# Row-LSTM over a group-normalised image: statistics laid out on 128 partitions, the first block's loads moved up among the first chunks, and the first row normalised on two other engines

## The chip, the cores and the metric

The kernel runs on one core of a Trainium2 chip. A core has a matrix engine (TensorE, PE in the profile; its weight loads are PEld), a vector engine (VectorE, DVE), an activation engine (ScalarE, ACT), a general engine (GpSimd, POOL) and a sync engine (SyncE, SP) that here only issues transfers. Sixteen DMA engines move data between the device memory (HBM) and the on-chip SBUF; PSUM takes the products of TensorE. Each engine works through its own instructions in order and waits on semaphores for the others. The metric is device time in microseconds (us); lower is better.

## The reference

The input `x` has shape (8, 96, 128, 128): batch, channels, rows, columns, in fp32. It is group-normalised, run row by row through a convolutional LSTM, and added to the result.

```python
def _gn(v, G=32, eps=1e-5):
    g = v.reshape(B_, G, C_ // G, H_, W_)
    m = jnp.mean(g, axis=(2, 3, 4), keepdims=True)
    s = jnp.var(g, axis=(2, 3, 4), keepdims=True)
    return ((g - m) / jnp.sqrt(s + eps)).reshape(v.shape)
...
its = conv(X, W_is * mask, padding=((0, 0), (1, 1))) + b_is       # 96 -> 384 channels, 3 wide, causal mask
def step(carry, row_in):                                          # over the 128 rows
    ss = conv(h, W_ss, padding=((1, 1),)) + b_ss                  # 96 -> 384 channels, 3 wide
    gates = ss + row_in
    ...
    c_new = f * c + i * g
    h_new = o * jnp.tanh(c_new)
...
x = x + _L0_conv_ref(_gn(x), ...)
```

Two facts matter here. The mean and the variance of a group (3 channels of one image, 49152 contiguous numbers) must be known before the first row can be normalised, so all 50.33 MB of `x` have to be read once before the recurrence starts. And the recurrence is serial: row r+1 needs the `h` of row r.

## The kernel before, in words

**Stage 1, statistics.** For each of the 8 images the kernel reads `x[b]` as 96 channels on 96 partitions, in 8 chunks of 2048 columns (768 KB, line 139, tile `xc`, 64 chunks in all). The chunks go through four buffers: the pool `x_pool` has the tags x0 and x1 with two buffers each. VectorE takes four `bn_stats` of 512 columns from each chunk (line 141, tile `bst`) and one `bn_aggr` for each image (line 142, tile `st`).

**Stage 2, from statistics to scale and shift.** Tiny products with the 0/1 matrix `gm` on TensorE (line 155) add the channels of a group and spread the sum to the partitions in the two layouts that are needed later; VectorE and ScalarE turn them into `rstd` and `nmr` (lines 158 to 172).

**Stage 3, the first block.** The batch is cut in two halves (s = 0 and 1, four images each) and the rows into blocks of R = 4. For each half and block `load_rows` reads channels 0 to 63 twice into `xr` (partitions 0 to 63, one float further on, and 64 to 127; lines 183 and 184, 512 KB each), and `load` reads channels 64 to 95 and 0 to 95 into an `x` tile (lines 189 and 190, 256 and 768 KB). SyncE issues these in program order behind the chunks. GpSimd then normalises the whole block of four rows, 8 instructions for each half (line 194: into `xn` from `xr`, and into the lower 32 partitions of `hx` from `x`), and clears a border column (line 213).

**Stage 4, the recurrence.** 128 rows times two halves give 256 half-steps. In a half-step TensorE makes 15 products in fp32 (line 270): six 256 columns wide on `vs` and `vf`, three 512 wide on `xn`, six 256 wide on `vd`. ScalarE copies and applies sigmoid and tanh, VectorE does the sums and gates and prepares `vs` and `vf` of the next row (lines 241 and 242), GpSimd prepares `vd` (line 243), adds the residual (line 332) and normalises the next block a little in each half-step. The two halves alternate so that the gates of one lie beside the products of the other.

**What sets the order.** From the `with tc.manual_schedule` on, TensorE, ScalarE, VectorE and GpSimd run their instructions in the order in which the code names them. Everything ahead of it is put in order by the framework's scheduler; SyncE's transfers keep program order on their queue. A DMA takes one of eight semaphores in turn and waits until the earlier DMA on that semaphore has landed.

Of the kernel before, what the change touches and what calls it, by code (L numbers as in the profile page):

```python
# [11 lines left out]
GROUPS = 32  # L12
# [9 lines left out]
def kernel(  # L22
# [38 lines left out]
    HW = H * W  # L61
    CH = R * BH * W
    SN = 512
    GSZ = C // GROUPS
# [43 lines left out]
    gm = const.tile([C, 2, P], F32, name="gm")  # L108
# [24 lines left out]
    st = const.tile([C, B, 2], F32, name="st")  # L133
    for b in range(B):
        bst = g_pool.tile([C, HW // SN, 6], F32, tag="bst", name=f"bst{b}")
        xb = x[b].rearrange("c h w -> c (h w)")
        for k in range(HW // CH):
            xc = x_pool.tile([P, CH], F32, tag=f"x{(b * (HW // CH) + k) % 2}", name=f"xc{b}_{k}")
            nc.sync.dma_start(xc[0:C], xb[:, bass.ts(k, CH)])
            for j in range(CH // SN):  # L140
                nc.vector.bn_stats(bst[:, k * (CH // SN) + j, :], xc[0:C, bass.ts(j, SN)])  # L141
        nc.vector.bn_aggr(st[:, b, :], bst.rearrange("c n s -> c (n s)"))


    mean = const.tile([P, 2, B], F32, name="mean")
    dq = const.tile([C, 2, B], F32, name="dq")
    v = const.tile([P, 2, B], F32, name="v")
    t1 = const.tile([P, 2, B], F32, name="t1")
    rstd = const.tile([P, 2, B], F32, name="rstd")
    nmr = const.tile([P, 2, B], F32, name="nmr")  # L150

    def grouped(src):
        pm = ps_st.tile([P, 2, B], F32, tag="pst", name="pm")
        for i in range(2):
            nc.tensor.matmul(pm[:, i, :], gm[:, i, :], src, start=True, stop=True)  # L155
        return pm

    nc.vector.tensor_copy(dq[:, 0, :], st[:, :, 0])  # L158
    nc.vector.tensor_scalar_mul(mean, grouped(dq[:, 0, :]), 1.0 / GSZ)
    nc.vector.tensor_sub(dq[:, 1, :], dq[:, 0, :], mean[0:C, 0, :])  # L160
    nc.vector.tensor_mul(dq[:, 1, :], dq[:, 1, :], dq[:, 1, :])
    nc.vector.tensor_add(dq[:, 1, :], dq[:, 1, :], st[:, :, 1])
    nc.vector.tensor_scalar(v, grouped(dq[:, 1, :]), 1.0 / GSZ, GN_EPS, ALU.mult, ALU.add)
    nc.scalar.activation(t1, v, AF.Sqrt)
    nc.vector.reciprocal(rstd, t1)

    nc.vector.tensor_mul(t1, rstd, rstd)
    nc.vector.tensor_mul(t1, t1, v)
    nc.vector.tensor_scalar(t1, t1, -0.5, 1.5, ALU.mult, ALU.add)
    nc.vector.tensor_mul(rstd, rstd, t1)  # L170
    nc.vector.tensor_mul(nmr, mean, rstd)
    nc.vector.tensor_scalar_mul(nmr, nmr, -1.0)  # L172


# [18 lines left out]
    def norm(dst, src, lo, layout, b):  # L193
        nc.gpsimd.tensor_scalar(  # L194
            dst,
            src,
            rstd[lo:P, layout, b : b + 1],
            nmr[lo:P, layout, b : b + 1],
            ALU.mult,
            ALU.add,  # L200
        )

    def normalise_own(s, k, j):

        i = k % 2
        norm(
            xn[s][i][:, :, :, j, :],
            xr[s][:, j, 0 : R * W].rearrange("p (r j t) -> p r t j", r=R, t=2),
            0,
            1,  # L210
            s * BH + j,
        )
        nc.gpsimd.memset(xn[s][i][0:C2, :, 0, j, 0:1], 0.0)

    def normalise_shared(s, k, j):

        norm(
            strided(
                hx[s][k % 2][C:P, 0, 0, j, :], 0, [(2 * BH * JP, R), (BH * JP + 1, 2), (1, J)]
            ),  # L220
            xt[s, k][C:P, j, :, :].rearrange("p r (j t) -> p r t j", t=2),
            C,
# [242 lines left out]
```

## Time and profile before

| what | value |
|---|---|
| median of three runs | 2238.5 us (2235.78 to 2239.08) |
| the profiled execution's own time | 2246.42 us |
| its span (first to last instruction) | 2244.6 us |
| instructions | 24459 |
| bytes read from HBM / written | 185.39 MB / 50.33 MB |
| busy share of the span | PE 89%, DVE 73%, PEld 64%, ACT 60%, POOL 46% |

The profile is one execution, taken by the hardware profiler. Its page shows each engine's busy share in 40 slices of about 56 us, the chain of work that ended last, and the costliest groups of instructions with what ended the idle time before them. A stretch can be looked at by itself: the table of stretches gives for each its length, the busy time of each engine with the count of instructions, the clock granted to TensorE, the mean busy share of the 16 DMA engines (1.00 and a little over mean that all are occupied all the time) and the rate in GB/s. The timeline gives instructions with their start and duration. Each fp32 product of the code is two MATMUL records.

### The profile page before, as it was taken

The numbers are of one execution on the slowest core, as the hardware profiler recorded it, in microseconds if no ns is written. First come the engines' busy times: TensorE is split into PE (matmuls) and PEld (weight loads), VectorE is DVE, ScalarE is ACT, GpSimd is POOL, SyncE is SP. The second block draws the span as 40 slices with busy tenths as digits, with TensorE's granted clock in tenths as the row PEclk, the third lists the DMA queues.
The fourth block names the chain that finished last, engine by engine and source line by source line (L and its number), as shares of the span: only waits on it lengthen the run. The fifth ranks groups of instructions, "written<-read, shape, count | busy, mean of one in ns | idle before, by whom it ended". The sixth has DMA issues, their size and how long they took to land.

```text
span 2244.6 us, 24459 instructions
## 1 busy us (share of the span) xinstructions
PE 2002.9 (89%) x7688; PEld 1441.8 (64%) x7688; DVE 1629.4 (73%) x3354; ACT 1348.8 (60%) x2564; POOL 1027.0 (46%) x1311
## 2 busy tenths in 40 slices
PE   0000899999999999999999999999999999999998
PEld 0000677777777777777777777777777777777775
DVE  6787577777777777777777777777777777777776
ACT  0000566666666666666666666666666666666665
POOL 0000545554555554455555555445555555544552
PEclk9999999999999999999999999999999999999999
DMA  9999544333334444433333444443333344444310
GB/s 237 242 246 236 101 104 104 89 81 81 81 83 104 104 103 104 104 85 84 79 80 87 104 104 103 103 104 85 81 81 79 89 104 104 104 103 104 85 48 28
DMA packets 103520, 237.30 MB, mean 106 GB/s; under 512 B 6560, under 2 KB 7136, under 8 KB 97248
## 3 DMA queue, kind: packets, MB, share of 16 engines
q1 hardware_dynamic: 102400, 234.91, 45.2%
q8 instruction: 62, 1.02, 0.2%
q10 hardware_dynamic: 992, 0.84, 0.2%
q14 instruction: 66, 0.54, 0.1%
HBM read 185.39 MB, written 50.33 MB: 105 GB/s over the span
## 4 chain that ended last, share of the span: by engine, by line
PE 89%; DMA 7%; DVE 3%; POOL 0%; issue 0%; ACT 0%; POOLq 0%; DVEq 0%
PE ps L270 89%; DMA xc<-in_x_dram 7%; DVE bst L141 2%; DMA wt<-in_w_ss_dram 0%; DMA wt<-in_w_is_dram 0%; POOL hx L194 0%; POOL xn L194 0%; PE pm L155 0%; POOLq L460 0%; POOL x L332 0%; DVE ps L287 0%; ACT L300 0%; ACT g L296 0%; ACT ps L300 0%; DVE ps L286 0%
## 5 line engine op out<-in xcount | busy, mean ns | idle before, releaser
L270 PEld LDWEIGHTS ps<-vd,wt 128*128 128x128 f32 x3072 | 583.7, 190 | 407.2 <-issue 366.9
L270 PE MATMUL ps<-xn,wt 128*128 128x512 f32 x1536 | 795.5, 599 | 0.0
L270 PE MATMUL ps<-vd,wt 128*128 128x256 f32 x3072 | 788.4, 379 | 0.0
L296 ACT ACTIVATE g<-ps 32x512 f32<-32x512 f32 x768 | 454.2, 591 | 466.3 <-PE ps L270 466.1
L243 POOL TENSOR_TENSOR vd<-hx 128x512 f32<-128x512 f32 x256 | 266.1, 1039 | 942.4 <-DVE vf L242 748.5
L280 ACT ACTIVATE m<-ps,bias 128x256 f32<-128x256 f32 x768 | 358.6, 467 | 184.1 <-PE ps L270 184.1
L270 PE MATMUL ps<-vs,wt 128*128 128x256 f32 x1536 | 458.5, 380 | 11.6 <-DVE vs L241 11.6
L270 PE MATMUL ps<-vf,wt 128*128 128x256 f32 x1536 | 458.2, 380 | 0.0
L300 ACT ACTIVATE ps<-ps 96x512 f32<-96x512 f32 x768 | 442.9, 577 | 16.1
L304 DVE TENSOR_TENSOR ps<-ps,c 96x512 f32<-96x512 f32 x256 | 177.9, 695 | 377.8 <-ACT ps L300 377.8
L287 DVE TENSOR_TENSOR ps<-m,ps 128x256 f32<-128x256 f32 x768 | 329.2, 429 | 26.4
L286 DVE TENSOR_TENSOR ps<-m,ps 128x256 f32<-128x256 f32 x768 | 324.3, 422 | 21.4 <-ACT m L280 5.4
L332 POOL TENSOR_TENSOR x<-x,hx 96x512 f32<-96x512 f32 x256 | 331.4, 1295 | 9.5 <-DVE hx L325 9.5
L270 PEld LDWEIGHTS ps<-vs,wt 128*128 128x128 f32 x1536 | 292.5, 191 | 52.0 <-DVE vs L241 12.1
L270 PEld LDWEIGHTS ps<-vf,wt 128*128 128x128 f32 x1536 | 292.7, 191 | 40.1
L270 PEld LDWEIGHTS ps<-xn,wt 128*128 128x128 f32 x1536 | 271.1, 189 | 73.1 <-DVE ps L287 32.0
L194 POOL TENSOR_SCALAR xn<-xr,rstd,nmr 128x512 f32<-128x512 f32 x256 | 208.1, 813 | 212.1 <-DVE nmr L172 212.1
L307 DVE TENSOR_TENSOR g<-ps,g 96x512 f32<-96x512 f32 x256 | 175.6, 686 | 106.7 <-ACT g L296 106.7
L194 POOL TENSOR_SCALAR hx<-x,rstd,nmr 32x512 f32<-32x512 f32 x256 | 207.7, 811 | 25.4
L155 PE MATMUL pm<-dq,gm 96*128 96x8 f32 x8 | 2.0, 362 | 220.0 <-DVE dq L158 219.1
L141 DVE BATCH_NORM_STATS2 bst<-xc 96x6 f32<-96x512 f32 x256 | 157.4, 675 | 40.5 <-DMA xc<-in_x_dram 40.5
L325 DVE TENSOR_TENSOR hx<-ps,th 96x512 f32<-96x512 f32 x256 | 173.9, 679 | 0.7 <-ACT th L315 0.7
(41 smaller groups left out, 596.6 us busy)
## 6 DMA issues: line engine op xcount, KB each, us to landing
xr<-in_x_dram SPq DMA_DIRECT2D x128, 512.0 KB, 9.3
xc<-in_x_dram SPq DMA_DIRECT2D x64, 768.0 KB, 10.3
x<-in_x_dram SPq DMA_DIRECT2D x64, 768.0 KB, 9.6
out_dram<-x SPq DMA_DIRECT2D x64, 768.0 KB, 5.3
x<-in_x_dram SPq DMA_DIRECT2D x64, 256.0 KB, 6.3
wt<-in_w_ss_dram ACTq DMA_DIRECT2D x2, 144.0 KB, 7.4
wt<-in_w_is_dram ACTq DMA_DIRECT2D x2, 96.0 KB, 6.3
wr<-in_w_ss_dram ACTq DMA_DIRECT2D x1, 144.0 KB, 8.9
```

Of the source, the lines that this page charges most:

```text
L141: nc.vector.bn_stats(bst[:, k * (CH // SN) + j, :], xc[0:C, bass.ts(j, SN)])
L194: nc.gpsimd.tensor_scalar(dst, src, rstd[lo:P, layout, b : b + 1], nmr[lo:P, layout, b : b + 1], ALU.mult, ALU.add,)
L243: diff = nc.gpsimd.tensor_sub(vd.rearrange("p t (b j) -> p t b j", b=BH), strided(h[:, 0, 0, :], 1, [(BH * JP - 1, 2), (JP, BH), (1, J)]), ...
L270: nc.tensor.matmul(o, wt[:, p, bass.ts(a, P)], rhs, start=start, stop=stop, skip_group_check=True)
L280: nc.scalar.activation(self.m1, self.ps[a][:, 0:HB], AF.Identity, bias=bias[:, a : a + 1])
L286: nc.vector.tensor_add(lo, self.m1, hi)
L287: nc.vector.tensor_sub(hi, self.m1, hi)
L296: nc.scalar.activation(self.g[a * 32 : (a + 1) * 32], self.ps[a][C:P], AF.Tanh)
L300: nc.scalar.activation(gate, gate, AF.Sigmoid)
L304: nc.vector.tensor_mul(f, f, cs[self.s].rearrange("p t b j -> p (t b j)"))
L307: nc.vector.tensor_mul(self.g, self.ps[1][0:C], self.g)
L332: nc.gpsimd.tensor_add(xo, xo, h)
```

## The change

Statistics. `x[b]` is read as a flat array cut into 128 equal pieces, one for each partition: a group is four neighbouring partitions, and an image is 6 chunks of 128 x 2048 (1 MiB), 48 chunks in all. The four chunk buffers are the first buffer of each `x_pool` tag and the two `xn` tiles of the odd blocks, which are not needed yet. After the fourth chunk the loads of the first block are issued. `bn_stats` and `bn_aggr` run on 128 partitions; `gm` has a third part, which gives the mean back to the 128 pieces.

First row. Row 0 of the first block is normalised ahead of rows 1 to 3: half 0 on VectorE, half 1 on ScalarE; rows 1 to 3 stay with GpSimd, behind the first `vd` of both halves. A sigmoid on one column, whose result nobody reads, comes right behind the square root.

Products that nobody reads. `spin(rows, count)` issues products 256 columns wide of the weight tile `wt` with itself, with 128, 64 or 32 rows; 112 of them stand ahead of the mean's products, ten behind the variance's.

```diff
-    gm = const.tile([C, 2, P], F32, name="gm")
+    gm = const.tile([P, 3, P], F32, name="gm")
...
-            xc = x_pool.tile([P, CH], F32, tag=f"x{(b * (HW // CH) + k) % 2}", name=f"xc{b}_{k}")
-            nc.sync.dma_start(xc[0:C], xb[:, bass.ts(k, CH)])
-                nc.vector.bn_stats(bst[:, k * (CH // SN) + j, :], xc[0:C, bass.ts(j, SN)])
...
+    ring = [
+        x_pool.tile([P, CH], F32, tag=f"x{s}", name=f"xs{s}") for s in range(NH)
+    ] + [xn[s][1].rearrange("p r t b j -> p (r t b j)") for s in range(NH)]
+    for b in range(B):
+        bst = g_pool.tile([P, QW // SN, 6], F32, tag="bst", name=f"bst{b}")
+        xb = x[b].rearrange("c h w -> (c h w)").rearrange("(p q) -> p q", p=P)
+        for k in range(QW // CH):
+            xc = ring[n % len(ring)]
+            n += 1
+            nc.sync.dma_start(xc, xb[:, bass.ts(k, CH)])
+            for j in range(CH // SN):
+                nc.vector.bn_stats(bst[:, k * (CH // SN) + j, :], xc[:, bass.ts(j, SN)])
+            if n == len(ring):
+                for s in range(NH):
+                    load_rows(s, 0)
+                    load(s, 0)
+        nc.vector.bn_aggr(st[:, b, :], bst.rearrange("c n s -> c (n s)"))
...
+    def spin(rows, count):
...
+        for i in range(count):
+            for q in range(P // rows):
+                at = bass.ds(q * rows, rows)
+                nc.tensor.matmul(
+                    banks[(q * rows // 32 + i % (rows // 32)) % 4][:, 0:256],
+                    wt[at, 0, 0:P],
+                    wt[at, 0, 0:256],
...
-    for s in range(NH):
-        load_rows(s, 0)
-        load(s, 0)
-    for s in range(NH):
-        for j in range(BH):
-            normalise_own(s, 0, j)
-            normalise_shared(s, 0, j)
-    for s in range(NH):
-        load_rows(s, 1)
-        load(s, 1)
-    moving = [inputs(s, 0) for s in range(NH)]
+    for count in (12, 4):
+        for rows in (P, 64, 32):
+            spin(rows, count)
     with tc.manual_schedule(engines={E.PE, E.Activation, E.DVE, E.Pool}):
+        for i in (2, 0, 1):
+            nc.tensor.matmul(pm[:, i, :], gm[:, i, :], st[:, :, 0], start=True, stop=True)
...
+        for i in range(2):
+            nc.tensor.matmul(pv[:, i, :], gm[:, i, :], dq, start=True, stop=True)
+        spin(P, 10)
...
+        nc.scalar.activation(t1, v, AF.Sqrt)
+        nc.scalar.activation(table, t1[:, 0, 0:1], AF.Sigmoid)
...
+        for s, engine in enumerate((nc.vector, nc.scalar)):
+            for j in range(BH):
+                normalise_shared(engine, s, 0, j, 0, 1)
+            for j in range(BH):
+                normalise_own(engine, s, 0, j, 0, 1)
+        for s in range(NH):
+            nc.vector.memset(xn[s][0][0:C2, 0, 0, :, 0:1], 0.0)
+            moving.append(inputs(s, 0))
+        for s in range(NH):
+            for j in range(BH):
+                normalise_shared(nc.gpsimd, s, 0, j, 1, R)
+            for j in range(BH):
+                normalise_own(nc.gpsimd, s, 0, j, 1, R)
+                border(nc.gpsimd, s, 0, j, 1, R)
+        for s in range(NH):
+            load_rows(s, 1)
+            load(s, 1)
```

**SyncE's transfers.** In the kernel before, the loads of the first block (`xr` and `x`, last eight rows here) stand behind the 64th chunk:

```order
L139 DMA xc_5_511<-in_x_dram 96x2048
L139 DMA xc_6_517<-in_x_dram 96x2048
L139 DMA xc_7_523<-in_x_dram 96x2048
L183 DMA xr_111<-in_x_dram 64x4x512
L184 DMA xr_111<-in_x_dram 64x4x512
L189 DMA x_0_558<-in_x_dram 32x4x512
L190 DMA x_0_558<-in_x_dram 96x4x512
L183 DMA xr_112<-in_x_dram 64x4x512
L184 DMA xr_112<-in_x_dram 64x4x512
L189 DMA x_0_563<-in_x_dram 32x4x512
L190 DMA x_0_563<-in_x_dram 96x4x512
```

After the change they stand behind the fourth chunk of 48 (the chunk buffers are `xs_129`, `xs_130`, `xn_108` and `xn_110`):

```order
L165 DMA xn_108<-in_x_dram 128x2048
L165 DMA xn_110<-in_x_dram 128x2048
L142 DMA xr_111<-in_x_dram 64x4x512
L143 DMA xr_111<-in_x_dram 64x4x512
L148 DMA x_0_155<-in_x_dram 32x4x512
L149 DMA x_0_155<-in_x_dram 96x4x512
L142 DMA xr_112<-in_x_dram 64x4x512
L143 DMA xr_112<-in_x_dram 64x4x512
L148 DMA x_0_160<-in_x_dram 32x4x512
L149 DMA x_0_160<-in_x_dram 96x4x512
L165 DMA xs_129<-in_x_dram 128x2048
L165 DMA xs_130<-in_x_dram 128x2048
```

So the fifth chunk is the thirteenth transfer of SyncE's queue, and nothing but chunks follows until the statistics end.

**GpSimd between the statistics and the recurrence.** Before, the four rows of half 0 (`xn_107`, `hx_103`) are normalised ahead of the first `vd`:

```order
L194 TENSOR_SCALAR xn_107<-xr_111,rstd,nmr 128x8x64 x2
L213 MEMSET xn_107 64x4
L194 TENSOR_SCALAR xn_107<-xr_111,rstd,nmr 128x8x64
L213 MEMSET xn_107 64x4
L194 TENSOR_SCALAR xn_107<-xr_111,rstd,nmr 128x8x64
L213 MEMSET xn_107 64x4 x2
L194 TENSOR_SCALAR hx_103<-x_0_558,rstd,nmr 32x4x2x64 x4
L243 TENSOR_TENSOR vd_0_602<-hx_103 128x512
```

After, VectorE has the first row of half 0 (half 1's stands on ScalarE in the same form), right behind the shift `nmr`:

```order
L403 TENSOR_SCALAR nmr<-nmr 128x16
L208 TENSOR_SCALAR hx_103<-x_0_155,rstd,nmr 32x2x64 x4
L208 TENSOR_SCALAR xn_107<-xr_111,rstd,nmr 128x2x64 x4
L413 MEMSET xn_107 64x4
L254 TENSOR_TENSOR vs_0_595<-hx_103 128x256
L255 TENSOR_TENSOR vf_0_596<-hx_103 128x256
L413 MEMSET xn_109 64x4
L254 TENSOR_TENSOR vs_0_602<-hx_105 128x256
```

Eight instructions of 128 columns on VectorE now stand where eight of 512 columns stood on GpSimd; GpSimd keeps the other three rows of both halves, behind its two `vd`.

**TensorE up to the first half-step**, after the change (the last two of the 112, the products for mean and variance, and the first two of the ten):

```order
L185 MATMUL spin_32_1_523<-wt 128x256
L185 MATMUL spin_32_1_524<-wt 128x256
L385 MATMUL pm<-st,gm 128x8 x3
L391 MATMUL pv<-dq,gm 128x8 x2
L185 MATMUL spin_128_0_554<-wt 128x256
L185 MATMUL spin_128_0_555<-wt 128x256
```

Before, `L155 MATMUL pm<-dq,gm 128x8 x4` is followed by the first real product, `vs` of half 0, directly; now that product comes behind the ten. The 112 need only the weight tile, which lands in the first microseconds; the ten stand between the variance's products and the first half-step.

115 lines of the change are left out of this document (59 added, 56 removed).

## The prediction, written before the result was known

> **What bounds the kernel now.** I read the page's slices first, then the chain of waits by engine.
>
> ```profile
> span 2244.6 us, 24459 instructions
> PE   0000899999999999999999999999999999999998
> DVE  6787577777777777777777777777777777777776
> DMA  9999544333334444433333444443333344444310
> PE 89%; DMA 7%; DVE 3%; POOL 0%; issue 0%; ACT 0%; POOLq 0%; DVEq 0%
> ```
>
> There are two kernels in one. From the fifth slice on TensorE is the chain; before it TensorE does nothing, the DMA engines are full, and VectorE is not. The table of stretches (length, busy time by engine, granted clock, DMA share, GB/s) puts numbers to both.
>
> ```profile
> core 0: us, PE busy (x) PEld busy (x) DVE busy (x) ACT busy (x) POOL busy (x), PEclk, DMA share, GB/s
> 1.00:2.00 1.00, 0.00 (x0) 0.00 (x0) 0.00 (x0) 0.00 (x0) 0.95 (x4) 1.00 0.69 98
> 20.00:200.00 180.00, 0.00 (x0) 0.00 (x0) 144.20 (x232) 0.00 (x0) 0.00 (x0) 1.00 1.02 246
> 400.00:1000.00 600.00, 600.00 (x2309) 432.13 (x2309) 439.19 (x924) 403.59 (x769) 306.07 (x383) 1.00 0.40 92
> ```
>
> Between 400 and 1000 us TensorE is busy for 600 of 600 us, and the change touches none of its products there. So the time can only move ahead of the recurrence. In the statistics all 16 DMA engines are occupied (1.02) and deliver 246 GB/s, while VectorE works 144 of 180 us: the transfers are the bound. The chain of waits shows the beat, four `bn_stats` in 2.48 us and then waiting for a chunk, and the timeline shows what follows the last chunk.
>
> ```profile
> 11.30 0.57 DVE wr L98
> 22.86 9.80 DMA xc<-in_x_dram
> 191.06 10.08 DMA xc<-in_x_dram
> 201.16 2.48 DVE bst L141 x4
> 215.30 2.48 DVE bst L141 x4
> 217.80 1.03 DVE st L142
> 219.07 1.02 PE L155 MATMUL pm<-dq,gm 96*128 96x8 f32 x4 [219.07 <-DVE dq L158]
> 220.13 0.17 DVE L159 TENSOR_SCALAR mean<-pm 128x16 f32<-128x16 f32 x1 [1.11 <-PE pm L155]
> 221.04 0.99 PE L155 MATMUL pm<-dq,gm 96*128 96x8 f32 x4 [0.95 <-DVE dq L162]
> 222.07 0.17 DVE L163 TENSOR_SCALAR v<-pm 128x16 f32<-128x16 f32 x1 [1.18 <-PE pm L155]
> 222.28 0.21 ACT L164 ACTIVATE t<-v 128x16 f32<-128x16 f32 x1 [210.06 <-DVE v L163]
> 223.65 0.17 DVE L171 TENSOR_TENSOR nmr<-mean,rstd 128x16 f32<-128x16 f32 x1
> 223.85 0.17 DVE L172 TENSOR_SCALAR nmr<-nmr 128x16 f32<-128x16 f32 x1
> 224.21 1.56 POOL L194 TENSOR_SCALAR xn<-xr,rstd,nmr 128x512 f32<-128x512 f32 x2 [212.12 <-DVE nmr L172]
> 231.17 0.43 DVE L241 TENSOR_TENSOR vs<-hx 128x256 f32<-128x256 f32 x1 [7.14 <-POOL hx L194]
> 231.65 1.22 PE L270 MATMUL ps<-vs,wt 128*128 128x256 f32 x2 [9.62 <-DVE vs L241]
> 236.93 1.27 PE L270 MATMUL ps<-xn,wt 128*128 128x512 f32 x2
> 237.67 1.28 ACT L296 ACT_TABLE_LOAD   x1
> 239.71 1.28 ACT L300 ACT_TABLE_LOAD   x1
> 244.52 0.70 PE L270 MATMUL ps<-vs,wt 128*128 128x256 f32 x2 [2.01 <-DVE vs L241]
> 252.47 0.59 PE L270 MATMUL ps<-vs,wt 128*128 128x256 f32 x2
> 252.90 0.59 PE L270 MATMUL ps<-vf,wt 128*128 128x256 f32 x2
> ```
>
> Call 217.8, the end of the last `bn_stats`, T. The aggregate, mean, variance and scale take until T + 6.2; GpSimd's eight normalisations until T + 13.4; the first half-step starts at T + 13.85, the second at T + 26.7 and the third at T + 34.7. The second to the third is 7.95 us; the first to the second is 12.87. In the first, six products take 231.65 to 236.93, 0.88 us each, where they later take 0.43 (252.47 to 252.90), although the granted clock reads 1.00 in every stretch shown; and ScalarE loads two tables of 1.28 us that the third half-step no longer has.
>
> **The change, part by part.** (1) *The rate of the chunks.* The same 50.33 MB come as 48 transfers of 1.049 MB over 128 partitions instead of 64 over 96. The engines are all occupied already, so is there anything to gain? The stretches of the first block's loads, which follow each other on one queue, answer that: in this order channels on partitions 0 to 63 (one float off), 64 to 127, 96 to 127, 0 to 95. The last row lies in the recurrence, where the only transfer left in flight is a store from 96 partitions, issued at 309.88.
>
> ```profile
> 210.30:213.80 3.50, 0.00 (x0) 0.00 (x0) 2.47 (x4) 0.00 (x0) 0.00 (x0) 1.00 1.05 167
> 213.80:216.30 2.50, 0.00 (x0) 0.00 (x0) 1.00 (x2) 0.00 (x0) 0.00 (x0) 1.00 1.07 211
> 216.30:217.60 1.30, 0.00 (x0) 0.00 (x0) 1.30 (x3) 0.00 (x0) 0.00 (x0) 1.00 1.07 200
> 217.60:221.00 3.40, 1.02 (x4) 0.92 (x4) 2.01 (x7) 0.00 (x0) 0.00 (x0) 1.00 1.08 236
> 319.50:320.00 0.50, 0.50 (x2) 0.19 (x1) 0.50 (x2) 0.50 (x1) 0.00 (x0) 1.00 1.05 410
> 309.88 0.59 SPq L335 DMA_DIRECT2D out_dram<-x  x1
> 321.88 0.32 SPq L189 DMA_DIRECT2D x<-in_x_dram  x1
> ```
>
> Every stretch has the engines full, and the rate goes from 167 to 410. So the share is not the limit: an engine's packets just take longer. 64 partitions of the upper half of SBUF get 211, and 32 of the same half get 200: it is the half that is worth about 205, not the count. 96 partitions, two thirds of whose bytes go to the lower half, could then get 205 x 3/2 = 308 and do get 236 to 246. 128 partitions load both halves alike: up to 2 x 205 = 410, which is also what the engines do in the store. The bounds are 246 (nothing gained) and 410; I take 400, since the halves' rows speak for the upper end.
>
> [...]
>
> (2) *When the statistics end.* Data start near 1.5 to 2 us. The first four chunks and the weights (4.2 + 0.9 MB) take 12.8 us at 400. Then come the eight loads of the first block, 4.19 MB, whose four rows above sum to 10.7 us for one half, 21 us for both; they used to run beside stages 1 to 3 and now hold up the fifth chunk. VectorE starts at about 11.3 us as before (its first instruction needs the weights), has done four chunks near 24 us, as in the row of 22.86, and waits until 2 + 12.8 + 21 + 2.6 + about 1 for landing = 39. From there 44 chunks go by the slower of two: VectorE, 2.48 + about 0.05 for the wait + a sixth of an aggregate (1.03 x 144/192 = 0.8, so 0.13) = 2.66; the transfers, 1.049/400 = 2.62. With 2.66, T becomes 39 + 117 = 156; with some unevenness between two such equal partners I take **157, a gain of 61** against 217.8. Four chunks may be in flight, 10 us of transfers against a landing time of about 2, so the ring doesn't bind.
>
> (3) *From T to the first product.* Aggregate 0.8; mean 1.6 (1.10 before with four records, now six of 0.25); up to the variance's products 0.9 and these 1.0 as before; to `nmr` 1.96 as before. Sum T + 6.3, against 6.2. Then eight instructions of 128 columns on VectorE: no row has that form; 16 columns go in steps of 0.21 (223.85 to 224.03), 256 in 0.43, so 1.7 to 3.4, and I take 1.7, as 128 columns are nearer to the small ones; border and `vs` 0.6. TensorE could start at T + 8.6, 5.3 earlier than before. The page has the two groups that price what ScalarE and GpSimd get.
>
> ```profile
> L280 ACT ACTIVATE m<-ps,bias 128x256 f32<-128x256 f32 x768 | 358.6, 467 | 184.1 <-PE ps L270 184.1
> L194 POOL TENSOR_SCALAR hx<-x,rstd,nmr 32x512 f32<-32x512 f32 x256 | 207.7, 811 | 25.4
> ```
>
> ScalarE loads the sigmoid's table (1.28) while VectorE works out `nmr`, then needs 8 x 0.34 (between the 0.21 of 222.28 and the 0.47 of a copy of 256 columns) for half 1, done by T + 9.1; half 1's first product is not due until T + 19, so this costs nothing, and the two table loads leave the first half-step. GpSimd's other 16 instructions (0.8 x 3/4 each, with eight borders, 11 us) end near T + 23; what queues behind them is `vd` of row 1, wanted near T + 30. The second block's `xr` waits for them and lands near T + 25 and T + 30, while GpSimd normalises it from T + 27 and T + 35. All this is covered by a few us each.
>
> (4) *The products that nobody reads.* The 112 wait for weights alone, so they run from about 9 us, at most 112 x 0.88 = 99 us, and are over long before T; they neither help nor hurt. The ten start at T + 4.3 and stand ahead of the real ones. If TensorE speeds up after 5.3 us of work, as in the rows of 231.65 and 236.93, six of them take 5.3 and four 1.7: the first real product moves from T + 8.6 to T + 11.3, but its half-step then runs without the slow six and takes about 7.85. Third half-step: 11.3 + 2 x 7.85 = T + 27.0. Without the ten: 8.6 + 5.3 + 5.2 + 7.9 = T + 27.0 too. They are worth nothing either way; if they stayed slow throughout, they would cost 1.6 more.
>
> [...]
>
> Sum: the third half-step stood at 217.8 + 34.7 = 252.5 and will stand at 157 + 27.0 = 184; **68.5 us** less, of them 61 from the statistics and 7.7 from the chain behind. All that follows is TensorE's own 7.8 us per half-step. The profiled execution took 2246.42 and would take 2178; its median is 7.9 lower (2238.5), so I forecast **2170 us**.
>
> **The rivals.** *Loads have a ceiling of their own.* No load in the rows above passes 246 and only a store shows 410; if each 32 partitions add what the step from 64 (205) to 96 (246) adds, 128 get 287. Then 44 chunks of 3.65 and the first four at that rate put T at 2 + 17.8 + 21 + 161 + 3.5 = 205.3: a gain of 12.5 + 7.7, 2218 us. For it: the 96-partition rate is 80% of what the halves allow. Against it: 32 and 64 partitions being equal. [...] *The rate stays, and the first block is in the way.* The place is SyncE's queue: if full engines mean 246 whatever the partitions, T = 2 + 20.7 + 21 + 187.5 + 3.5 = 235, 17 later, less 7.7 from the chain: 2248, slower. It decides below a rate of about 260, where the chunks no longer pay for the 21 us. For it: the share of 1.02; against it: the 410. *The chain behind the statistics gains nothing*, because two engines now normalise beside GpSimd, which slows VectorE's eight, and the ten stay slow: 2178 with the forecast's statistics; this lies inside the range.
>
> **How the numbers follow.** Forecast (a rate of 360 or more, the chain's rival included) 0.72, 2160 to 2185; the ceiling 0.18, 2183 to 2218; the kept rate 0.10, 2230 to 2250. I leave out the last and the upper part of the ceiling: 2160 to 2206. About 0.2% (4.5 us) is what can be told from no change here. Faster takes the first two cases, 0.90; the third splits into 0.02 the same and 0.08 slower.
>
> **What would show it.** Right: `bn_stats` without waits from about 40 us on, a rate near 390 there, an idle VectorE between 24 and 39 us, the last `bn_stats` near 157, the first real product 11 us later at the fast pace, two table loads ahead of it. Wrong: a rate below 300 with the share still at 1.0 (a ceiling), a fifth chunk that lands after 45 us (the first block slower than its rows), or a gap on TensorE in the first ten half-steps (GpSimd or `xr` late).

## The result, and the profile after

| kernel | median of its runs | span of the profiled execution | its own time |
|---|---|---|---|
| before | 2238.28 us (2235.78 to 2239.08, 4 runs) | 2244.6 | 2246.42 |
| changed | 2173.69 us (2172.96 to 2174.94, 4 runs) | 2171.9 | 2173.67 |

The ratio is 0.9714 with a 95% interval of 0.9697 to 0.9731: the change makes the kernel 64.6 us faster, and the time is 3.7 above the forecast of 2170. The page of the changed kernel, slices and chain of waits:

```profile
span 2171.9 us, 24875 instructions
PE   4019999999999999999999999999999999999998
DVE  4987777777777777777777777777777777777776
PEclk8559999999999999999999999999999999999999
DMA  9991444333444443334444332344443334444411
PE 92%; DVE 0%; issue 0%; POOLq 0%; POOL 0%; ACT 0%
```

Before, TensorE's digits rose in the fifth slice; now they rise at the end of the third, from about 154 us on. The 4 in its first slice are the products that nobody reads. Behind that the page is the old one. The table of stretches has the first block's loads and then the chunks:

```profile
18.00:34.00 16.00, 13.12 (x168) 10.99 (x164) 4.78 (x9) 0.00 (x0) 0.00 (x0) 1.00 1.06 213
...
60.00:120.00 60.00, 0.00 (x0) 0.00 (x0) 59.86 (x101) 0.00 (x0) 0.00 (x0) 0.50 1.01 420
```

At the same share of about 1.0 the engines deliver 213 GB/s to the first block and 420 to the chunks, where the kernel before had 246. VectorE is busy for 59.86 of 60 us: it and the transfers are now bounds together. The timeline from the first chunk behind the first block to the third half-step (its columns are start, duration, engine, line, and in brackets the idle time and who ended it):

```profile
41.51 4.97 DVE L167 BATCH_NORM_STATS2 bst<-xs 128x6 f32<-128x512 f32 x8 [18.73 <-DMA xs<-in_x_dram]
142.20 4.83 DVE L167 BATCH_NORM_STATS2 bst<-xs 128x6 f32<-128x512 f32 x8
150.50 2.48 DVE L167 BATCH_NORM_STATS2 bst<-xn 128x6 f32<-128x512 f32 x4 [1.09 <-DMA xn<-in_x_dram]
153.87 1.45 PE L385 MATMUL pm<-st,gm 128*128 128x8 f32 x6 [122.75 <-DVE st L172]
157.07 6.28 PE L185 MATMUL spin<-wt 128*128 128x256 f32 x20
159.23 0.17 DVE L398 TENSOR_TENSOR t<-rstd 128x16 f32<-128x16 f32 x1 [1.26 <-ACT table L395]
160.49 1.51 DVE L208 TENSOR_SCALAR hx<-x,rstd,nmr 32x128 f32<-32x128 f32 x4
162.02 1.12 DVE L208 TENSOR_SCALAR xn<-xr,rstd,nmr 128x128 f32<-128x128 f32 x4
163.75 0.67 PE L283 MATMUL ps<-vs,wt 128*128 128x256 f32 x2 [0.39 <-DVE vs L254]
171.88 0.59 PE L283 MATMUL ps<-vs,wt 128*128 128x256 f32 x2
179.73 0.59 PE L283 MATMUL ps<-vs,wt 128*128 128x256 f32 x2
```

VectorE waits 18.73 us for the fifth chunk and has its last statistics at 150.50 + 2.48 = 153.0. This is T; it was 217.8. The first real product stands at T + 10.8, the third half-step at T + 26.75 = 179.73, where it stood at 252.47: 72.7 us earlier, which is the difference of the two spans. The medians differ by 64.6 only. The experiment on the kernel before shows where half of the other 8 went, and bears on the rest.

### The profile page after: what moved, and what is told of

Read it like the earlier page. It is cut to its first block, busy times and chain, and to the rows that moved or that the text cites. A ratio compares the mean times of both kernels' runs of the same rounds, so it can differ in the third digit from the quotient of the medians.

```text
span 2171.9 us, 24875 instructions
## 1 busy us (share of the span) xinstructions
PE 2030.3 (93%) x7934; PEld 1465.1 (67%) x7934; DVE 1588.7 (73%) x3299; ACT 1351.5 (62%) x2572; POOL 1028.0 (47%) x1311
## 3 DMA queue, kind: packets, MB, share of 16 engines
HBM read 185.49 MB, written 50.33 MB: 109 GB/s over the span
## 4 chain that ended last, share of the span: by engine, by line
PE 92%; DVE 0%; issue 0%; POOLq 0%; POOL 0%; ACT 0%
PE ps L283 92%; DVE hx L208 0%; POOLq L508 0%; POOL x L345 0%; DVE ps L300 0%; DVE ps L299 0%; DVE xn L208 0%; DVE hx L338 0%; DVE c L324 0%; ACT m L293 0%; DVE vs L254 0%; DVE nmr L402 0%; DVE rstd L401 0%; DVE nmr L403 0%; DVE t L399 0%
## 5 line engine op out<-in xcount | busy, mean ns | idle before, releaser
L313 ACT ACTIVATE ps<-ps 96x512 f32<-96x512 f32 x768 | 442.9, 577 | 16.1
L208 POOL TENSOR_SCALAR hx<-x,rstd,nmr 32x512 f32<-32x512 f32 (+1 forms) x256 | 207.9, 812 | 25.4
L208 POOL TENSOR_SCALAR xn<-xr,rstd,nmr 128x512 f32<-128x512 f32 (+1 forms) x256 | 208.3, 814 | 0.2
L324 DVE TENSOR_TENSOR c<-ps,g 96x512 f32<-96x512 f32 x256 | 173.9, 679 | 0.0
L328 ACT ACTIVATE th<-c 96x512 f32<-96x512 f32 x256 | 157.9, 617 | 0.9 <-DVE c L324 0.9
```

What stands on the lines that cost most here:

```text
L208: engine.tensor_scalar(dst, src, scale, shift, ALU.mult, ALU.add)
L313: nc.scalar.activation(gate, gate, AF.Sigmoid)
L324: nc.vector.tensor_add(c, self.ps[0][0:C], self.g)
```

## The experiments

All kernels below compute the whole result, and none leaves work out. The diffs are excerpts: `...` marks what is left out, and the comments in them are added here. Where nothing else is said, the edit is made on the changed kernel, and a ratio is against the kernel before in runs of the same chip.

### The layout alone

The kernel before with the statistics on 128 partitions (48 chunks, the four old buffers), and nothing else of the change: the first block stays behind the chunks and with GpSimd, and there are no unread products.

```diff
-            nc.sync.dma_start(xc[0:C], xb[:, bass.ts(k, CH)])
+            nc.sync.dma_start(xc, xb[:, bass.ts(k, CH)])      # xb = x[b] as 128 equal pieces
```

> The kernel before with the statistics on 128 partitions and nothing else: chunks through its own four buffers, first block behind the last chunk, GpSimd normalising the whole block, no unread products. Theory (the layout alone lifts the rate from 246 to about 418 GB/s, VectorE becomes the bound): last bn_stats near 135 us, third half-step 34.7 us later as before, so 170 us against 252 before and 180 in the changed kernel: 2164 us, faster than the whole change. Rival (the layout gives the 61 to 65 us of the statistics stage only together with the early block): 2178 to 2182 us.

Measured: 2165.05 us (2164.35 to 2165.95), ratio 0.9661 (0.9638 to 0.9683). From its timeline, the last statistics and the first two half-steps:

```profile
133.62 2.47 DVE L142 BATCH_NORM_STATS2 bst<-xc 128x6 f32<-128x512 f32 x4 [2.68 <-DMA xc<-in_x_dram]
150.16 1.22 PE L271 MATMUL ps<-vs,wt 128*128 128x256 f32 x2 [9.62 <-DVE vs L242]
162.28 0.70 PE L271 MATMUL ps<-vs,wt 128*128 128x256 f32 x2 [2.08 <-DVE vs L242]
```

T is 136.1, 16.9 earlier than in the whole change, and the second half-step follows at T + 26.2, as late behind T as before (26.7). So the layout by itself gives more than the whole change does. What the other edits gain behind T (the second half-step at T + 18.9 instead of T + 26.2, 7.3 us) is less than the 16.9 us that the early first block costs ahead of it. The spans agree: 2171.9 - 2162.6 = 9.3, and 16.9 - 7.3 = 9.6.

### Half of the layout undone

Everything of the change stays, but the chunks go to 96 partitions again.

```diff
-            nc.sync.dma_start(xc, xb[:, bass.ts(k, CH)])
+            nc.sync.dma_start(xc[0:C], xb[:, bass.ts(k, CH)])     # 64 chunks, 96 partitions
```

> The changed kernel with the statistics back on 96 partitions (64 chunks of 768 KB); early block, first row on VectorE and ScalarE and unread products stay. Theory (the rate hangs on the partitions): 246 GB/s again, 60 chunks of 3.2 us behind the fifth's landing near 41 us, last bn_stats near 233 us, 2246 to 2254 us, slower than the kernel before by 0.3 to 0.7%. Rival (the gain comes from the other parts, or the rate from the ring of buffers): under 2200 us.

Measured: 2253.64 us (2252.32 to 2261.13), ratio 1.0063 (1.0041 to 1.0086): 0.6% slower than the kernel before. One stretch of its table, and the start of the mean's products:

```profile
60.00:120.00 60.00, 0.00 (x0) 0.00 (x0) 48.77 (x79) 0.00 (x0) 0.00 (x0) 0.50 1.02 250
```

```profile
233.25 1.42 PE L386 MATMUL pm<-st,gm 128*128 128x8 f32 x6 [199.59 <-issue]
```

With 250 GB/s the mean's products start at 233.25 instead of 153.87. This is the prediction's rival of the kept rate (T = 235, 2248), made real: with it the first block is in the way and the change loses. So the 128 partitions carry the gain of the statistics; what the other edits give behind T does not make up for the early block without them.

### Which partitions, how fast

Loads that nobody reads go ahead of the statistics: rows of 8 KB, one form after the other.

```diff
+    forms = ((0, 64, 8), (64, 128, 8), (32, 96, 8), (0, 96, 8), (0, 128, 8), (96, 128, 16))
+    for lo, hi, count in forms:
+        for i in range(count):
+            nc.sync.dma_start(ring[i % len(ring)][lo:hi], part[lo:hi, bass.ts(i % 6, CH)])
```

> The changed kernel with loads that nobody reads ahead of the statistics, rows of 8 KB as in the chunks, 8 of each form one after the other (16 of the last): partitions 0 to 63, 64 to 127, 32 to 95, 0 to 95, 0 to 127, 96 to 127. Theory of the prediction (the half of the partitions carries about 205, not the count): 0 to 63 and 64 to 127 at 200 to 215 GB/s, 96 to 127 at 200, and 32 to 95, whose two halves get 32 partitions each, at 350 to 420, since both halves are loaded alike; 0 to 95 at 250, 0 to 127 at 415. Rival (the count of partitions carries the rate, and 32 to 95 is one more form of 64): 32 to 95 at 200 to 215. Second rival (each 32 partitions add a share of their own): 96 to 127 near 100, which the 200 of the first block's loads already speaks against.

Measured: one run of 2296.02 us; the added 122 are these loads. One stretch inside each form, in that order (the last two columns are the share of the DMA engines and GB/s):

```profile
18.00:22.00 4.00, 4.00 (x59) 3.54 (x59) 0.00 (x0) 0.00 (x0) 0.00 (x0) 1.00 1.04 209
38.00:42.00 4.00, 0.00 (x0) 0.00 (x0) 0.00 (x0) 0.00 (x0) 0.00 (x0) 0.50 1.00 201
50.00:54.00 4.00, 0.00 (x0) 0.00 (x0) 0.00 (x0) 0.00 (x0) 0.00 (x0) 0.50 1.03 387
66.00:70.00 4.00, 0.00 (x0) 0.00 (x0) 0.00 (x0) 0.00 (x0) 0.00 (x0) 0.50 1.01 229
94.00:98.00 4.00, 0.00 (x0) 0.00 (x0) 0.00 (x0) 0.00 (x0) 0.00 (x0) 0.50 1.01 418
118.00:122.00 4.00, 0.00 (x0) 0.00 (x0) 0.00 (x0) 0.00 (x0) 0.00 (x0) 0.50 0.97 199
```

The third row decides: 64 partitions that lie half in each half of SBUF get 387, and 64 partitions within one half get 201 to 209. In these rows the halves carry the rate, not the count: 32 partitions of one half (the last row, 199) get about as much as 64 of it. The first three forms have transfers of the same size, and all six take their rows from `x` cut into the same 128 pieces, so neither the size of a transfer nor the way in which HBM is read makes the difference. The share of the DMA engines tells none of this: it reads 0.97 to 1.04 in the six rows. What the theory of halves does not give is the rate of 96 partitions: by an estimate from the rows of 201 to 209, two thirds of the bytes at 205 would allow 308, and 229 to 250 are measured. That stays open.

### The first block behind the chunks

```diff
-            if n == len(ring):
-                for s in range(NH):
-                    load_rows(s, 0)
-                    load(s, 0)
         nc.vector.bn_aggr(st[:, b, :], bst.rearrange("c n s -> c (n s)"))
+    for s in range(NH):
+        load_rows(s, 0)
+        load(s, 0)
```

> The loads of the first block are issued behind the last chunk instead of behind the fourth; nothing else differs from the changed kernel. Theory (the 21 us of first-block transfers ahead of the fifth chunk are paid in full, because VectorE, which is the bound at 2.53 us a chunk, stands idle for 18.7 us): the idle time goes, the last bn_stats ends near 135 us instead of 153; ScalarE then waits some 3 us for half 1's loads ahead of the copies of the first half-step. Net 15 us less: 2159 us, between 2155 and 2164. Rival (the block has to be read some time, and the place in the queue does not matter): 2174 us within 2.

Measured: 2165.62 us (2164.04 to 2167.47), ratio 0.9662 (0.9635 to 0.969), 6.6 more than expected and outside the range. A row of VectorE, of ScalarE and of TensorE:

```profile
133.85 2.47 DVE L167 BATCH_NORM_STATS2 bst<-xn 128x6 f32<-128x512 f32 x4 [1.81 <-DMA xn<-in_x_dram]
150.77 2.06 ACT L205 ACTIVATE hx<-x,nmr,rstd 32x128 f32<-32x128 f32 x4 [8.23 <-DMA x<-in_x_dram]
156.23 2.04 PE L282 MATMUL ps<-xn,wt 128*128 128x512 f32 x2 [6.32 <-issue]
```

T comes down to 136.3 as expected. But ScalarE, which has half 1's row 0 ahead of the first half-step's copies, now waits 8.23 us for half 1's `x`, the last transfer of the block. The copies `m` stand behind it on ScalarE, VectorE's sums wait for them, and TensorE stands still for 6.32 us in its first half-step. The saving of 16.7 was real, and some 9 of it (the half-step lasts 17.3 instead of 8.1) went into a new wait on an engine that the prediction had covered.

### The same, with the waits taken away

The loads that row 0 does not need go last, half 1's row 0 moves to GpSimd behind the first half-step's sums, and the unread sigmoid reads `v` instead of `t1`.

```diff
+    for s in range(NH):
+        load_rows(s, 0)
+        load_low(s, 0)          # channels 64 to 95, for hx
+    for s in range(NH):
+        load_own(s, 0)          # channels 0 to 95, for the residual
...
-        nc.scalar.activation(table, t1[:, 0, 0:1], AF.Sigmoid)
+        nc.scalar.activation(table, v[:, 0, 0:1], AF.Sigmoid)
...
+                if not prev:
+                    second_half()   # row 0 of half 1 and rows 1 to 3 of both, on GpSimd
```

> The changed kernel with the first block's loads behind the last chunk, in another order: both halves' transfers to the upper partitions and to xr first, the two of 96 partitions, which row 0 of the first products does not need, last; half 1's row 0 is normalised by GpSimd behind the first half-step's sums instead of by ScalarE, and the unread sigmoid reads v, so that VectorE does not wait for it. Theory (the late block is worth 16.7 us of statistics, and the 9 us that it lost with ScalarE waiting for half 1's x come from that wait alone): T = 136.3, first real product near T + 10, third half-step near T + 26, 2173.7 - 16.7 - 1.3 = 2155.7, range 2153 to 2158. Rival (the transfers of the late block are in the way of the first rows whatever their order, since 21 us of transfers end at T + 15 or later): 2162 to 2167, with TensorE waiting between the first and the third half-step.

Measured: 2157.63 us (2157.45 to 2157.81), ratio 0.9639 (0.9624 to 0.9654).

```profile
146.15 0.59 PE L291 MATMUL ps<-vs,wt 128*128 128x256 f32 x2
166.90 1.13 PE L291 MATMUL ps<-vd,wt 128*128 128x256 f32 x4 [1.39 <-POOL vd L264]
```

T is 135.6. The first real product stands at 146.15, and nothing stops TensorE up to the third half-step; there a new wait of 1.39 us, for a `vd` that GpSimd has behind its other rows, is most of the 1.9 above the 2155.7. So the theory holds: T is 17.4 earlier than in the changed kernel, and once nobody waits for the block's last transfer nearly all of it arrives. The 16.1 us (2173.69 - 2157.63) belong to the three edits together; they were not taken apart.

### The weights prepared later

The kernel of the last experiment, with the sums of the weights moved from the start of VectorE into its waits behind the statistics, and the 112 unread products gone.

```diff
-    nc.vector.tensor_add(wr[:, 0, :], wt[:, 0, :], wt[:, 3, :])
...
-    for count in (12, 4):
-        for rows in (P, 64, 32):
-            spin(rows, count)
...
         for i in (2, 0, 1):
             nc.tensor.matmul(pm[:, i, :], gm[:, i, :], st[:, :, 0], start=True, stop=True)
+        nc.vector.tensor_add(wr[:, 0, :], wt[:, 0, :], wt[:, 3, :])
```

> The kernel of e9_late_order with one more change: the sums that prepare the weights stand behind the last chunk's statistics in VectorE's waits, and the 112 unread products are gone. Theory (VectorE starts when the first chunk has landed, near 5 us instead of 11, and the transfers, 50.33 MB at about 415 GB/s, become the pace): T between 129 and 134, total 2 to 5 us below e9_late_order, 2150 to 2154. Rival (VectorE is the pace of all 48 chunks, and an earlier start only moves its waits): T as in e9_late_order within 1.5 us and the total within 1.5 us of it.

Measured: 2156.63 us (2156.6 to 2156.7), ratio 0.9634 (0.9619 to 0.9649): 1.0 less than the last one, outside the theory's range and within the rival's 1.5.

```profile
6.89 2.47 DVE L169 BATCH_NORM_STATS2 bst<-xs 128x6 f32<-128x512 f32 x4 [6.89 <-DMA xs<-in_x_dram]
15.79 4.95 DVE L169 BATCH_NORM_STATS2 bst<-xn 128x6 f32<-128x512 f32 x8 [2.61 <-DMA xn<-in_x_dram]
132.08 2.47 DVE L169 BATCH_NORM_STATS2 bst<-xn 128x6 f32<-128x512 f32 x4 [2.70 <-DMA xn<-in_x_dram]
```

VectorE starts at 6.89 instead of 11.7, and gives most of the lead back in waits for chunks, 2.61 us at the third and 2.70 at the last; T is 134.6, 1.0 earlier. The transfers are the other bound, right behind it.

### One more step, for the best version

Three edits on the last kernel: the weights' transfers named behind the fourth chunk, eight unread products instead of ten, and rows 1 to 3 of half 1 behind half 0's `vd`.

```diff
+            if n > len(ring) and late:
+                nc.scalar.dma_start(*late.pop(0))     # one weight transfer with each chunk
...
-        spin(P, 10)
+        spin(P, 8)
...
+                    if (prev.s, prev.row) == (0, 0):
+                        other_rows(1)
```

> The kernel of e10_prep_later with three more changes: the transfers of the weights go behind the fourth chunk, one with each chunk, so that the third and fourth chunk are not issued behind them; eight unread products instead of ten; rows 1 to 3 of half 1 behind half 0's vd of row 1 on GpSimd. Theory (e10_prep_later is bound by its transfers, which delivered 272 GB/s in the first 10 us and 352 in the next 10, and then 420; filled stretches are worth up to 10 x 148/420 + 10 x 68/420 = 5.1 us, less what VectorE cannot follow, since it works without a wait for most of the statistics): T 2 to 4 us earlier, first product 0.8 earlier behind it, TensorE's 1.2 us of waiting for vd gone: 2156.6 - 4 to 6 = 2150.5 to 2152.5. Rival (VectorE's own work, 48 x 2.43 + 7 x 0.73 = 121.7 behind the first chunk at 6.9, is the bound): T no earlier than 133, and 2154 to 2155.

Measured: 2154.62 us (2153.88 to 2155.58), ratio 0.9618 (0.9595 to 0.9641), above the theory's range and inside the rival's.

```profile
0.74 0.43 ACTq L170 DMA_DIRECT2D wt<-in_w_ss_dram  x1
132.74 2.47 DVE L172 BATCH_NORM_STATS2 bst<-xn 128x6 f32<-128x512 f32 x4 [2.68 <-DMA xn<-in_x_dram]
144.74 0.67 PE L291 MATMUL ps<-vs,wt 128*128 128x256 f32 x2 [0.17 <-DVE vs L262]
```

The first edit did nothing: ScalarE's queue still issues the weights from 0.74 us on, since nothing on it waits, so whether earlier chunks would help was not tested, and the rival's number does not decide for its cause. T is 135.2, not earlier. The 2 us come from the other two: the first product at T + 9.5 instead of T + 10.9, with the eight over in time, and no wait for `vd`. This is the fastest version, 19 us below the changed kernel.

### The unread products

First without any, then without the 112 alone.

```diff
-    for count in (12, 4):
-        for rows in (P, 64, 32):
-            spin(rows, count)
...
-        spin(P, 10)
```

> The changed kernel without any of the products that nobody reads. My prediction's sum: no difference, 2173.7 us within 1. Rival, from the changed kernel's trace (the ten end at 163.0 us, just ahead of the first real product at 163.75, which then runs at the fast pace): without them the first six products take 0.88 us each again and the first half-step 10.9 us instead of 8.1, 2176.4 us within 1.

> The changed kernel without the 112 unread products; the ten stay. Theory (the 112 are over 120 us before the first real product and touch no clock that matters; all of the 2.2 to 2.6 us that were lost without any unread product belong to the ten): 2173.7 +- 0.7, first product at the fast pace again, third half-step near 179.7. Rival (the 112 set a state of TensorE that lasts, and the ten alone do not reach it): 2175.5 to 2176.5, third half-step near 181.9.

Measured: 2176.30 us (2175.91 to 2177.22) without any, ratio 0.9711 (0.9689 to 0.9734); 2174.83 us (2174.13 to 2175.48) without the 112, ratio 0.9717 (0.9698 to 0.9735). First the products without any, from the mean to the third half-step, then those without the 112:

```profile
154.18 1.45 PE L382 MATMUL pm<-st,gm 128*128 128x8 f32 x6 [154.18 <-DVE st L172]
163.95 1.22 PE L283 MATMUL ps<-vs,wt 128*128 128x256 f32 x2 [6.42 <-DVE vs L254]
164.96 1.06 PE L283 MATMUL ps<-vf,wt 128*128 128x256 f32 x2
181.91 0.59 PE L283 MATMUL ps<-vs,wt 128*128 128x256 f32 x2
```

```profile
154.28 1.45 PE L382 MATMUL pm<-st,gm 128*128 128x8 f32 x6 [154.28 <-DVE st L172]
164.14 0.67 PE L283 MATMUL ps<-vs,wt 128*128 128x256 f32 x2
172.28 0.59 PE L283 MATMUL ps<-vs,wt 128*128 128x256 f32 x2
```

Without any, the first product starts 9.8 us behind the mean's, and with the ten 9.9: the ten delay nothing, as VectorE is not ready earlier. But they take the slow phase on themselves, in which a product 256 columns wide takes 1.06 us and not 0.59: the third half-step is 25.9 us behind the mean's products with them, and 27.7 without, 1.9 more. That is the rival's number (2176.4), and not the prediction's "no difference". Without the 112 the first half-step runs at the fast pace, and the second follows after 8.14, as in the changed kernel (8.13). The 112 do nothing for the products. The median of 2174.83 lies just outside the theory's 2174.4; 0.4 of the 1.1 us to the changed kernel is a later T, and the rest is too close to the spread of the runs to be told.

### The whole first block on GpSimd

Row 0 goes back to GpSimd with the rest of its block. In the first version half 1's `vs` was named ahead of the first half-step, as the changed kernel has it; in the second behind that half-step's sums.

```diff
-        for s, engine in enumerate((nc.vector, nc.scalar)):
-            for j in range(BH):
-                normalise_shared(engine, s, 0, j, 0, 1)
...
+                normalise_own(nc.gpsimd, s, 0, j, 0, R)
```

> The changed kernel with the whole first block normalised by GpSimd, as in the kernel before. Theory (the first half-step then starts 12 to 13 us behind nmr's products instead of 8; the ten are over 6 us before it, so that the first six products are slow again): first real product at T + 14 instead of T + 10.8, slow ones cost 2.5 more, 2173.7 + 3.2 + 2.5 = about 2179.5, range 2178 to 2183. Rival (GpSimd's late first row is hidden, as the third half-step is set by something else): 2173 to 2175.

> The changed kernel with the whole first block normalised by GpSimd, as in e6_pool, but with half 1's row prepared behind the first half-step's sums, so that VectorE does not wait for GpSimd ahead of them (in e6_pool TensorE stood still for 5.9 us for that). Theory: the first real product at T + 15.5, as in e6_pool, against T + 10.8 in the changed kernel, its first six products slow again (2.6): 4.7 + 2.6 = 7.3 above the changed kernel, 2181, range 2179 to 2184. Rival (what e6_pool lost is the normalisation itself and not the order): 2187 to 2190 again.

Measured: 2189.19 us (2188.51 to 2190.11), ratio 0.978 (0.9764 to 0.9796), for the first; 2180.48 us (2180.13 to 2180.86), ratio 0.9734 (0.9707 to 0.9761), for the second. The first missed its range. Its rows of VectorE and TensorE show why:

```profile
179.95 0.43 DVE L254 TENSOR_TENSOR vs<-hx 128x256 f32<-128x256 f32 x1 [8.52 <-POOL hx L208]
181.62 2.05 PE L283 MATMUL ps<-xn,wt 128*128 128x512 f32 x2 [5.93 <-issue]
```

VectorE waited 8.52 us for half 1's `hx` with the first half-step's sums queued behind that wait, and TensorE stood still for 5.93. It had been put there by the experiment's own order, and its T was 2.7 later too. The second version has neither, and its total lies where the theory put it:

```profile
168.87 0.67 PE L283 MATMUL ps<-vs,wt 128*128 128x256 f32 x2 [4.08 <-DVE vs L254]
169.37 0.59 PE L283 MATMUL ps<-vf,wt 128*128 128x256 f32 x2
170.45 1.06 PE L283 MATMUL ps<-vf,wt 128*128 128x256 f32 x2
178.38 0.59 PE L283 MATMUL ps<-vs,wt 128*128 128x256 f32 x2
```

So row 0 on the two other engines is worth 6.8 us (2180.48 - 2173.69; the spans differ by 6.4): 4.8 by starting earlier behind the mean's products (14.7 with GpSimd, 9.9 now), 1.4 because the first half-step, 9.5 long with GpSimd and 8.1 now, has no slow products, and 0.3 by T. The first product at T + 15.6 is the theory's; the products at the slow pace cost 1.4 and not its 2.6, because the first two still ran at the fast pace. Row 0 also goes ahead of the other three rows there, and whether that or the other engines give the gain was not tested apart.

### The kernel before, once more

> The kernel before, profiled once more: the first profiled execution took 2246.42, 8 above the median of its runs, and the prediction took that distance over to the changed kernel. Theory (the distance lies in the transfers of the statistics, which bound the kernel before and vary from run to run): an execution of 2236 to 2242 has its last statistics 4 to 10 us earlier than 217.8, at a rate of 249 to 252 GB/s, and the same 26.7 us from there to the second half-step. Rival (it lies in the recurrence or outside the span): the last statistics within 2 us of 217.8.

Measured: 2239.19 us (2235.69 to 2246.71, 10 runs), ratio 1.0004 (0.9991 to 1.0017); the profiled execution's span is 2240.4. Its statistics as a stretch, and the two rows that bound the way from T to the second half-step:

```profile
20.00:200.00 180.00, 0.00 (x0) 0.00 (x0) 147.44 (x237) 0.00 (x0) 0.00 (x0) 1.00 1.02 251
```

```profile
211.11 2.47 DVE L141 BATCH_NORM_STATS2 bst<-xc 96x6 f32<-96x512 f32 x4 [2.29 <-DMA xc<-in_x_dram]
240.28 0.70 PE L270 MATMUL ps<-vs,wt 128*128 128x256 f32 x2 [2.01 <-DVE vs L241]
```

T is 213.6 here and was 217.8; the spans are 2240.4 and 2244.6. Both differ by 4.2, and from T to the second half-step it is 26.7 both times. The whole distance between the two executions lies ahead of T, where the transfers went at 251 GB/s and at 246; over 50.33 MB that is 4.1 us. The executions of this kernel spread over 11 us (10 runs), and over 8.8 when the changed kernel's chunks go to 96 partitions. With chunks on 128 partitions no kernel here spreads over more than 3.5, the layout alone over 1.6 (4 runs each).

## Why the prediction was right, and where it was not

**The rate of the chunks** was right, and for its reason. 400 was taken and 420 measured, the ceiling of 287 did not show, and the loads of partitions 32 to 95 show the halves (387 GB/s, against 201 to 209 for as many partitions of one half). One piece of its evidence was weaker than its use: the store's 410 was the highest of its stretches of half a microsecond, and those beside it read 336 and 348. For two edges of its chances, a rate of 360 for the forecast and 2183 us for the ceiling, no run shows a source; the runs show chunks at 420 GB/s in the changed kernel and at 419 with the layout alone, both from 60 to 120 us.

**The end of the statistics** was 157 in the sum and is 153.0, from two terms that were off in opposite directions. The fifth chunk came at 41.5 instead of 39: the first 20 us moved 273 and then 296 GB/s instead of 400, and SyncE issued the third chunk only at 10.85. And VectorE's beat is (153.0 - 41.5)/44 = 2.53 and not 2.66: the 2.48 of four `bn_stats` came from chunks that VectorE had waited for. Back to back, eight take 4.83 in the row of 142.20 and the next ones begin after 4.75, so that four cost 2.4.

**The offset to the median** is the step that failed most. The prediction took the 7.9 us between the profiled execution of before and its median over to the changed kernel. The second profile of before puts 4.2 of them into its transfers. It is itself 3.0 above the median of its runs; that the rest lies there too is not shown directly, but only kernels with chunks on 96 partitions spread so far. The changed kernel has no such distance (2173.67 and 2173.69). Its sum for the profiled execution was 2178; the third half-step came 4.3 earlier than its 184, and 2178 - 4.3 is the time measured. The forecast of 2170 lies as near as it does because 7.9 too much was taken off and 4.3 too little; that is luck.

**The chain from T** ends right, at T + 26.75 against 27.0, through steps that are not. `nmr` came at T + 7.4 and not 6.3: the unread sigmoid reads `t1`, which VectorE overwrites next, so VectorE waits 1.26 us for ScalarE's table. The prediction had said that the table load hides, and had not asked who waits for the instruction that brings it. Taken away in the kernels with the sigmoid on `v`, it frees that time: `nmr` is done at T + 6.2 in the fastest of them. The eight normalisations took 1.51 + 1.12 = 2.63 and not 1.7, the lower of the two bounds. In the kernel without the ten TensorE starts at T + 10.7 (163.95, with T at 153.3) and not at T + 8.6. The sum came out right because it let the ten hold TensorE until T + 11.3, which covers that delay.

**The ten products** were "worth nothing either way" and are worth 1.9 us by the trace. That the first of them are slow in place of the real ones was right, but not that this only pays for their own time. VectorE was 2.1 us later than the sum had it, and the ten were shorter: 6.28 us instead of 7.0, about four products at the slow pace and six at the fast one, by an estimate from 0.86 and 0.43 us from one product to the next. So they were over at T + 10.4, just before VectorE. That they fit is in part luck, since the same ten last 6.78 us without the 112 and 7.44 with GpSimd's first row. In the kernel with the sigmoid on `v` they were about 1 late, and eight were enough. That the 112 cost nothing was right.

**The covers** held: no table load stands in the first half-step (the last one ahead of it is at 157.70, 1.28 us long), and no gap of TensorE shows in the first ten (it is busy for 8.06 of the first one's 8.13 us, and for all 70.12 us from there to 242). Two proved thin when an experiment moved work: ScalarE's row 0 as soon as the first block came late, and GpSimd's `vd` by 1.4 us once half 1's row was added to it.

**What the sum did not ask** is whether the first block should go first at all. The prediction priced its 21 us on the way and set them against the faster chunks, but not against leaving the block behind them. With the layout in place they cost 17 us of T, and the layout alone runs at 2165.05 us, 8.6 below the whole change.

## What to carry to other kernels

DMA engines that read as full, at shares of 1.00 to 1.04, delivered 201 to 209 GB/s here to 64 partitions of one half and 387 to 64 over both: lay a load over both halves of the partitions before anything else is moved, and read the GB/s beside the share. Transfers put ahead of the bound queue of chunks cost 16.7 us of T here, so look first whether they can go last, in the order in which they are needed, with no engine waiting in program order for the last of them. And add a profile's own distance to its median to a forecast only when it is known which stage it comes from.

## What the runs showed of the hardware

The granted clock did not always tell the pace of TensorE. Here is one stretch from each of three kernels: the changed kernel's ten products, the first real products without any unread ones, and those with GpSimd's first row:

```profile
157.00:162.00 5.00, 5.00 (x17) 4.15 (x17) 2.88 (x12) 3.09 (x6) 0.00 (x0) 0.64 0.14 41
```

```profile
164.00:168.40 4.40, 4.40 (x11) 3.50 (x12) 2.58 (x7) 1.56 (x4) 3.06 (x4) 1.00 0.00 0
```

```profile
170.00:172.00 2.00, 2.00 (x6) 1.62 (x5) 0.86 (x2) 0.92 (x2) 1.90 (x4) 0.50 0.46 84
```

In the first and the third the slow products stand under 0.50, as one would read it; the 0.64 is a mean of 0.50 up to about 160.5 us and 1.00 behind it. In the second the same slow products (1.06 us) stand under 1.00. What sets the two apart ahead of T is the 112. With them TensorE works for 23.76 us, from 7.36 to 31.1, and then falls idle; the record reads 1.00 up to 34 us, 0.64 in the next one and 0.50 from 35 us until T. Without any unread products it reads 1.00 from 60 to 120 us, and from 154 until the products are fast. The kernel that lacks only the 112 shows this too: 1.00 from 157 to 162 us, with 14 records of TensorE there where the changed kernel has 17. The kernel before lacks them as well: from 231.6 to 236 us, where its products take 1.06 us, the record reads 1.00, which is what the prediction found.

The fall to 0.50 also comes late. With GpSimd's first row the ten end at 164.8, TensorE then idles for 4.08 us, and its first two products are still fast (168.87 and 169.37 are 0.50 apart); from about 170 on, 5 us behind the start of the pause, four are slow, though TensorE is at work by then. Nor is the slow phase of one length, as the ten show: 6.28, 6.78 and 7.44 us in three kernels.

And 96 partitions, of which a store reached 410 GB/s for half a microsecond in the prediction's row, load at 229 to 251 in all three kernels that do it. Neither the halves nor the count explains that.
